# One core, two attention parts: the end of the global part handed to the local part piece by piece

## The chip, the cores and the metric

The kernel runs on one core of a Trainium2 chip. Its time is device microseconds per execution, the median of a few; the profile is one more execution, taken with the hardware profiler. Engines are named as the profile names them: PE (TensorE, matmuls and transposes), DVE (VectorE), ACT (ScalarE), POOL (GpSimd), SP (SyncE, which issues most DMAs). All data is float32.

## What is computed

For x of shape (2, 2048, 256), with `ln` the layer normalization without weights:

```python
xn  = ln(x)
s   = global_attention(xn) + ln(xn) * gamma + beta   # 16 heads of 16, a spatial bias on 256 keys, softmax over 2048
g   = silu(ffn(xn))                                  # two layers, below
out = x + s * g
# one ffn layer: shift half of the channels by one token; q, k, v = h @ wqkv (8 heads of 64);
# l2norm and rotary on q, k; attention in windows of 128 with the window before;
# x += o @ wo; shift, layer norm, h @ w1, a * gelu(g), x += h @ w2
```

The global part (s) and the local part (g) both read xn. The last step multiplies them.

## The kernel before

`gated_recurrent_kernel` first calls `global_attention` (L152), then `ffn_branch` (L792). Each opens its own pools of tiles in SBUF and its own pool of the eight PSUM banks (`ps_r` at L167, `ps_f` at L804), and inside each the order of work is written out by hand: what the functions emit is what the engines' queues get, in that order.

**The global part** works through 32 units (batch, group of four heads, 512 queries) in periods of `PATTERN`: tiles of maxima (P, L419 with DVE's L422), of scores (S, L463 with ACT's exponential at L465), sums over values (V, L481) and single pieces of other work (X), taken from the list `others`. Behind the last period three things are left for the last unit: `sums` turns the sums and divides them by their row sum (transposes pd, L564; DVE L567 and L575), `turn_back` turns them back (transposes pr, L584; ACT copy oc, L586), and `project` is called twice (matmuls px, L592; DVE adds them to s at L597, and behind the second SP sends s to DRAM, L599). L684 runs what remains of `others`.

**The local part** goes over 64 tiles of 128 tokens (16 slots of 512), layer by layer. Before its first tile it clears on POOL `u_last` (L814), two `k_ring` (L817) and six `sm` (L820), whose zeros at the edges are read later, and loads weights (`load_o`, `load_1`, `load_2`, L1207 to L1209). In step n the order of pieces is a list of letters, `FIRST_STEP` for n up to 8 and then `STEP`:

- Q, K, V: the projections of tile n (L889). For Q and K DVE multiplies by rotary tables (L906 to L908), ACT squares (sqq, L910), POOL adds (L911); one piece later DVE sums the squares (L915, L919) and POOL takes the root by a power (L920) and scales (L921). For V ACT copies (L895).
- T0, T1: the turning of Q and K of tile n - 1 (transposes L934; ACT copies xT at L938, DVE copies K into `k_ring` at L943).
- S0, S1: the scores of tile n - 1 (L962; DVE masks and takes maxima at L976, ACT exponentials at L984; one piece later the scaling, for the first eight tiles on ACT, L995).
- W0, W1, A0, A1: the weights of tile n - 2 turned (L1013; copies pT at L1019) and the sums over values (L1036; ACT copies oT, L1044).
- R, F, G: pieces of the feed-forward block of earlier slots (L1051, L1067 to L1091, L1127 and on).

`bank` hands out the eight PSUM banks in turn. `load_tables` (L709) loads the rotary tables of a slot on SP and multiplies them by scales on POOL (L718); for the first layer it is called at the start of steps 1, 3 and 5.

Of the kernel before, what the change touches and what calls it, by code (L numbers as in the profile page):

```python
# [11 lines left out]
F32 = mybir.dt.float32  # L12
# [6 lines left out]
P = 128  # L19
# [23 lines left out]
@with_exitstack  # L43
def gated_recurrent_kernel(ctx: ExitStack, tc: tile.TileContext, t: dict, out: bass.AP):
    nc = tc.nc

    xf = t["x"].rearrange("b n d -> (b n) d")
    x_ch = xf.rearrange("(c t p) d -> c p t d", t=TPC, p=P)
    out_ch = out.rearrange("b n d -> (b n) d").rearrange("(c t p) d -> c p t d", t=TPC, p=P)

    const = ctx.enter_context(tc.tile_pool(name="const", bufs=1))


    ident = const.tile([P, P], F32, name="ident")
    make_identity(nc, ident)
    eps_t = const.tile([P, 1], F32, name="eps_t")
    nc.gpsimd.memset(eps_t, EPS)
    mean_w = const.tile([P, P], F32, name="mean_w")
    nc.gpsimd.memset(mean_w, 1.0 / D)

    vecs = const.tile([P, DEPTH, 2 * NM + 6], F32, name="vecs")
    b2_row = const.tile([P, D], F32, name="b2_row")


    xA = [const.tile([P, 2, N + 1], F32, name=f"xA{b}") for b in range(B)]
    for b in range(B):
        nc.gpsimd.memset(xA[b][:, :, 0:1], 0.0)
    dram = ctx.enter_context(tc.tile_pool(name="dram", bufs=1, space=bass.MemoryType.DRAM))
    s_out = [dram.tile([P, TPC, D], F32, name=f"s_out{c}") for c in range(B * NCH)]

    s_pool = ctx.enter_context(tc.tile_pool(name="s", bufs=1))
    weights = ffn_weights(tc, t, const, s_pool)
    early = [
        lambda: nc.sync.dma_start(vecs, t["vecs"]),
        lambda: nc.sync.dma_start(b2_row, t["b2"][DEPTH - 1 : DEPTH, :].to_broadcast([P, D])),
    ] + [lambda: weights[1](0), lambda: weights[3](0), lambda: weights[2](0, 0)]

    s_all = [s_pool.tile([P, NT, D], F32, tag=f"s{b}", name=f"s{b}") for b in range(B)]
    global_attention(tc, t, xA, s_all, s_out, ident, eps_t, x_ch, early)
    ffn_branch(tc, t, xA, s_out, weights, ident, eps_t, mean_w, vecs, b2_row, x_ch, out_ch)  # L80


# [68 lines left out]

def global_attention(tc, t, xA, s_all, s_out, ident, eps_t, x_ch, early):  # L152

# [10 lines left out]
    with ExitStack() as ctx:  # L164
        cp = ctx.enter_context(tc.tile_pool(name="ga_c", bufs=1))
        p2 = ctx.enter_context(tc.tile_pool(name="ga_2", bufs=2))
        psr = ctx.enter_context(tc.tile_pool(name="ps_r", bufs=1, space=PSUM))  # L167

# [60 lines left out]
        nc.gpsimd.memset(mhalf, -0.5)  # L229
        wp = cp.tile([P, NPR, D], F32, name="wp")  # L230
        for h in range(NG * GH):
# [9 lines left out]
        rings = dict(FIRST_RINGS)  # L241

        def bank(name, shape=(P, CH), ring=None):
            ring = ring or other_ring[0]
            turn[ring] += 1
            tags = rings[ring]
            return psr.tile(list(shape), F32, tag=tags[turn[ring] % len(tags)], name=name)
# [97 lines left out]
        qkv = {}  # L345

        def prep_qk(pi, n, c):
            b, pr = divmod(pi, NPR)
            ps = bank(f"pp_{pi}_{c}_{n}")
            for k in range(2):  # L350
                nc.tensor.matmul(  # L351
                    ps, w[n][:, k, pr * P : (pr + 1) * P], xA[b][:, k, 1 + c * CH : 1 + (c + 1) * CH],
                    start=(k == 0), stop=(k == 1),
                )
            st = p2.tile([P, CH], F32, tag="stage", name=f"stage_{pi}_{c}_{n}", bufs=2)
            nc.scalar.activation(st, ps, AF.Copy, scale=HD ** -0.5 if n == "wq" else 1.0)
            qk_d[pi, n, c] = dram.tile([P, CH], F32, name=f"qk_{pi}_{n}_{c}")
            nc.sync.dma_start(qk_d[pi, n, c], st)
# [113 lines left out]
        def sum_piece():  # L472
# [12 lines left out]
            if kt == 0:  # L485
                os[n] = p2.tile([P, CH], F32, tag="o", name=f"o_{n}")
                nc.scalar.copy(os[n], po)
# [31 lines left out]
        def spread_sums(n, o):  # L519
# [6 lines left out]
            if r == 0:  # L526
                ocs[key] = p2.tile([P, CH], F32, tag=f"on{qc}", name=f"oc_{b}_{g // 2}_{qc}", bufs=1)
            for j in range(GH):
# [30 lines left out]
        def sums(n, o):  # L559
# [3 lines left out]
            for i in range(TPC):  # L563
                nc.tensor.transpose(ps[:, i, :], o[:, i * P : (i + 1) * P], ident)  # L564
            rd = p2.tile([P, TPC, GH, 1], F32, tag="rd", name=f"rd_{n}")
            po = ps.rearrange("p i (j d) -> p i j d", d=HP)
            nc.vector.reciprocal(rd, po[:, :, :, HD : HD + 1])  # L567
            if g % 2 == 0:
                ons[b, g, qc] = p2.tile(
                    [P, TPC, PH, HD], F32, tag=f"on{qc}", name=f"on_{b}_{g // 2}_{qc}", bufs=1  # L570
                )
            on = ons[b, g - g % 2, qc]
# [8 lines left out]
        def turn_back(b, pr, qc, on):  # L581
            ps = bank(f"pr_{b}_{pr}_{qc}")
            for i in range(TPC):
                nc.tensor.transpose(ps[:, i * P : (i + 1) * P], on[:, i].rearrange("p h d -> p (h d)"), ident)  # L584
            o = p2.tile([P, CH], F32, tag="stage", name=f"oc_{b}_{pr}_{qc}", bufs=2)
            nc.scalar.copy(o, ps)  # L586
            others[:0] = [lambda: project(b, pr, qc, o, 0), lambda: project(b, pr, qc, o, 2)]
# [94 lines left out]
        while waiting:  # L682
            pass_place()
        while others:  # L684
            others.pop(0)()

# [94 lines left out]


STEP = "T0 T1 W0 W1 S0 S1 A0 A1 R Q K V F G G G".split()

FIRST_STEP = "Q T0 W0 W1 T1 R K A0 A1 S0 G S1 V F G G".split()
N_FIRST = 8
N_SM = 6
# [3 lines left out]

def ffn_branch(tc, t, xA, s_out, weights, ident, eps_t, mean_w, vecs, b2_row, x_ch, out_ch):  # L792

# [7 lines left out]
    with ExitStack() as ctx:  # L801
        cp = ctx.enter_context(tc.tile_pool(name="ff_c", bufs=1))
        pool = ctx.enter_context(tc.tile_pool(name="ff", bufs=2))
        psr = ctx.enter_context(tc.tile_pool(name="ps_f", bufs=1, space=PSUM))  # L804

# [7 lines left out]
        u_last = cp.tile([P, CH], F32, name="u_last")  # L813
        nc.gpsimd.memset(u_last, 0.0)  # L814
        k_ring = [cp.tile([P, 4, 3 * P], F32, name=f"k_ring{b}") for b in range(B)]
        for k in k_ring:
            nc.gpsimd.memset(k[:, :, P : 2 * P], 0.0)  # L817
        sms = [cp.tile([P, 2, 2 * HD2 + WIN], F32, name=f"sm{i}") for i in range(N_SM)]
        for sm in sms:
            nc.gpsimd.memset(sm, 0.0)  # L820
        next_sm = [0]
        ctx.enter_context(tc.manual_schedule())

        turn = [0]

        def bank(name, shape=(P, CH)):
            turn[0] += 1
            return psr.tile(list(shape), F32, tag=f"f{turn[0] % 8}", name=name)

# [254 lines left out]
        def f_var(s):  # L1084
# [3 lines left out]
            nc.tensor.matmul(pw, mean_w, sq[:, 0, :], start=True, stop=True)  # L1088
            rs = pool.tile([P, CH], F32, tag="rs", name=f"rs_{s}", bufs=1)
            def root():  # L1090
# [16 lines left out]
        def f_var_at(s, n, places):  # L1107
# [3 lines left out]
            for (dn, op), f in zip(places, todo):  # L1111
                hook(n + dn, op, f)

        def f_gate(s, m, n):

# [14 lines left out]
            if n == 1:  # L1130
                gl = pool.tile([P, CH], F32, tag="gl", name=f"gl_{nm}")
                nc.scalar.activation(gl[:mw], ps[:mw], AF.Gelu, bias=V[:mw, NM + m : NM + m + 1])  # L1132
# [8 lines left out]
        def f_last(s, m, mw):  # L1141
# [5 lines left out]
            for k in range(2):  # L1147
                nc.tensor.matmul(ps, W["1 last"][:, k, :], hc[:, k, :], start=(k == 0), stop=(k == 1))
            gl = pool.tile([P, CH], F32, tag="gl", name=f"gl_{s}_{m}")
            h = P // 2  # L1150
# [6 lines left out]
        def f_out(s, k, part):  # L1157
# [16 lines left out]
            if part == 0:  # L1174
                F["py"] = bank(f"pz_{s}_{k}", (P, 2, D))
                F["xt"] = bank(f"pzx_{s}_{k}", (P, 2, D))
                F["s"] = pool.tile([P, 2, D], F32, tag="s", name=f"s_{s}_{k}", bufs=1)
                F["x"] = pool.tile([P, 2, D], F32, tag="x", name=f"x_{s}_{k}", bufs=1)
                F["y"] = pool.tile([P, 2, D], F32, tag="y", name=f"y_{s}_{k}")
                nc.sync.dma_start(F["s"], s_out[b * NCH + cc][:, 2 * k : 2 * k + 2, :])  # L1180
# [25 lines left out]
        gates = []  # L1206
        load_o(0)  # L1207
        load_1(0)
        load_2(0)  # L1209
# [13 lines left out]
        for n in range(len(tiles) + 4):  # L1223
            s, i = divmod(n, TPC)
            cur, pre, pre2 = (tiles[x] if 0 <= x < len(tiles) else None for x in (n, n - 1, n - 2))
            order = FIRST_STEP if n <= N_FIRST else STEP

# [29 lines left out]
            if i == 0 and s % B == 0 and B <= s <= per_layer:  # L1257
                if s == B:
                    load_scales(1)
                load_tables(1, s // B - 1)  # L1260
            if n in (1, 3, 5):
                load_tables(0, (n + 1) // 2)
            if i == 0 and s == per_layer:
# [8 lines left out]
            for op in order:  # L1272
# [7 lines left out]
                elif op[0] in "WA":  # L1280
                    if pre2:
                        piece(lambda: (a_weights if op[0] == "W" else a_sums)(*pre2, j))
                elif op == "R":
                    if i == 0 and have(s - 2):
# [14 lines left out]
                for f in hooks.pop((n, op), []):  # L1299
                    f()  # L1300

            if s == per_layer and i == 1:
                load_o(1)
# [112 lines left out]
```

## Time and profile before

| what | value |
| --- | --- |
| median of three runs | 3050.07 us (3047.15 to 3050.91) |
| the profiled execution's own time | 3048.12 us |
| its span, first to last instruction | 3046.3 us |
| mean granted TensorE clock | 0.991 |
| busy: PE, DVE, ACT, POOL | 2972.1, 2198.3, 2131.6, 1609.2 us |
| last transposes pd of the global part | 1678.05 us |
| its last matmuls px | 1680.92 us |
| first projection of the local part | 1683.69 us |
| first transposes of the local part | 1693.63 us |

Times of day in the text are microseconds from the span's start. In the profile's lines "out<-in" names tiles; L is the line of the kernel; "A <- B" in a list of waits means that A stood idle until B was done. PE's records of a float32 matmul come in pairs, two for an instruction. A busy PE is not a PE at its peak.

### The profile page before, as it was taken

How to read it: one execution, taken by the hardware profiler on the slowest of the kernel's cores; microseconds unless marked ns; L12 is line 12 of the kernel's file. 1: busy time of each engine (PE TensorE's matmuls, PEld its weight loads, DVE VectorE, ACT ScalarE, POOL GpSimd, SP SyncE). 2: the span in 40 equal slices, each digit the busy share in tenths (PEclk: the TensorE clock that was granted, in tenths of full speed). 3: DMA queues.
4: the chain of work that ended last, by engine and by line, in shares of the span. 5: the costliest groups of instructions: out<-in, count | busy, mean ns of one | idle time of the engine just before them, and what ended most of it. 6: DMA issues, size and time to landing. Idle time of an engine off the chain costs nothing.

```text
span 3046.3 us, 60013 instructions
## 1 busy us (share of the span) xinstructions
PE 2972.1 (98%) x22348; PEld 1340.3 (44%) x22348; DVE 2198.3 (72%) x4792; ACT 2131.6 (70%) x4524; POOL 1609.2 (53%) x1454
## 2 busy tenths in 40 slices
PE   8999999999999999999999889999999999999998
PEld 3433333333333333333333455555555555555565
DVE  6898888788887788888884556666666666666653
ACT  3788878788887788888888565555555655665652
POOL 3575435456543354444542746656666556666642
PEclk9999999999999999999999989999999999999999
DMA  3100101000001100000000200000000000000001
GB/s 121 30 14 18 28 19 30 26 12 21 21 25 45 50 19 14 14 25 7 7 10 27 71 10 1 8 1 8 1 29 8 1 21 17 22 22 22 22 22 55
DMA packets 65847, 70.62 MB, mean 23 GB/s; under 512 B 28744, under 2 KB 44188, under 8 KB 65556
## 3 DMA queue, kind: packets, MB, share of 16 engines
q1 hardware_dynamic: 64658, 66.00, 7.2%
q8 instruction: 177, 2.90, 0.4%
q14 instruction: 114, 0.93, 0.1%
q10 hardware_dynamic: 386, 0.52, 0.0%
q0 software_dynamic: 512, 0.26, 0.0%
HBM read 45.26 MB, written 17.53 MB: 21 GB/s over the span
## 4 chain that ended last, share of the span: by engine, by line
PE 88%; DVE 3%; ACT 3%; issue 3%; POOL 1%; DMA 1%; SPq 0%; POOLq 0%; DVEq 0%; ACTq 0%
PE pm L419 18%; PE po L481 16%; PE ps L463 14%; PE pp L889 10%; PE pg L1127 7%; PE po L1036 3%; PE px L1051 3%; PE ps L962 3%; PE py L1166 3%; PE pz L1185 2%; PE pw L1013 1%; ACT sm L984 1%; PE px L592 1%; PE pp_wk L351 1%; PE pv L385 1%
## 5 line engine op out<-in xcount | busy, mean ns | idle before, releaser
L422 DVE TENSOR_REDUCE mx<-pm 128x1 f32<-128x512 f32 x2048 | 1270.3, 683 | 218.0 <-PE ps L463 207.3
L465 ACT ACTIVATE e<-ps 128x512 f32<-128x512 f32 x2048 | 1058.2, 603 | 246.2 <-PE ps L463 245.5
L419 PE MATMUL pm<-kT,qT 32*128 32x512 f32 x4096 | 1020.0, 616 | 4.8 <-DVE mx L422 4.6
L463 PE MATMUL ps<-qa,kT 32*128 32x512 f32 x4096 | 1013.1, 615 | 0.0
L493 POOL TENSOR_TENSOR o<-o,part 128x512 f32<-128x512 f32 x465 | 589.5, 1268 | 777.4 <-ACT part L492 772.4
L419 PEld LDWEIGHTS pm<-kT,qT 32*128 32x128 f32 x4096 | 402.7, 183 | 409.9 <-DVE mx L422 385.2
L481 PE MATMUL po<-e,v 128*32 128x512 f32 x4096 | 546.3, 605 | 0.0
L463 PEld LDWEIGHTS ps<-qa,kT 32*128 32x128 f32 x4096 | 397.1, 183 | 187.1 <-ACT e L465 107.3
L998 POOL TENSOR_TENSOR sm<-sm,wls 128x384 f32<-128x384 f32 x224 | 180.3, 826 | 396.7 <-DVE wls L990 389.0
L889 PE MATMUL pp<-weights,xA 128*128 128x512 f32 x768 | 357.0, 613 | 0.8 <-DVE s L597 0.8
L492 ACT COPY part<-po 128x512 f32<-128x512 f32 x465 | 287.0, 617 | 6.4 <-PE po L481 5.2
L1127 PE MATMUL pg<-hc,weights 128*128 128x512 f32 x640 | 284.8, 592 | 0.0
L481 PEld LDWEIGHTS po<-e,v 128*32 128x32 f32 x4096 | 81.0, 108 | 389.4 <-ACT e L465 359.8
L984 ACT ACTIVATE sm<-sm,wmx 128x192 f32<-128x192 f32 x512 | 225.4, 441 | 6.1 <-DVE wmx L976 5.5
L920 POOL TENSOR_TENSOR rn<-rn,mhalf 128x8 f32<-128x8 f32 x128 | 215.6, 1684 | 15.1 <-DVE rn L919 10.9
L889 PEld LDWEIGHTS pp<-weights,xA 128*128 128x128 f32 x768 | 143.7, 193 | 170.3 <-issue 167.9
L910 ACT ACTIVATE sqq<-pp 128x512 f32<-128x512 f32 x128 | 76.3, 596 | 176.9 <-DVE swp L908 148.2
L1127 PEld LDWEIGHTS pg<-hc,weights 128*128 128x128 f32 x640 | 121.1, 190 | 150.2 <-issue 145.7
L911 POOL TENSOR_TENSOR rot<-rot,swp 128x512 f32<-128x512 f32 x128 | 163.3, 1289 | 31.0 <-DVE swp L908 30.9
L1136 DVE SCALAR_TENSOR_TENSOR u<-pg,vecs,gl 128x512 f32<-128x512 f32 x80 | 59.9, 748 | 151.4 <-ACT gl L1132 74.2
L976 DVE CUSTOM_DVE_ANT_0 sm<-ps,mask 128x192 f32<-128x192 f32 x512 | 147.0, 352 | 3.1 <-PE ps L962 2.7
L990 DVE RECIPROCAL wls<-wls 128x4 f32<-128x4 f32 x128 | 22.8, 178 | 174.4 <-ACT sm L984 174.3
(177 smaller groups left out, 3409.8 us busy)
## 6 DMA issues: line engine op xcount, KB each, us to landing
s<-in_x_dram SPq DMA_DIRECT2D x8, 512.0 KB
qk_wk<-stage_wk SPq DMA_DIRECT2D x16, 256.0 KB
kT<-qk_wk SPq DMA_DIRECT2D x128, 32.0 KB
qk_wq<-stage_wq SPq DMA_DIRECT2D x16, 256.0 KB
qT<-qk_wq SPq DMA_DIRECT2D x128, 32.0 KB
qa<-qk_wq SPq DMA_DIRECT2D x128, 32.0 KB
s_out<-s SPq DMA_DIRECT2D x8, 512.0 KB
s<-s_out SPq DMA_DIRECT2D x16, 256.0 KB
```

Source lines behind the costliest of these rows:

```text
L419: nc.tensor.matmul(ps, qT[rows, q0 : q0 + P], kT[rows, c * CH : (c + 1) * CH], start=True, stop=True)
L422: nc.vector.tensor_reduce(mxs[n][:, j * TPC + i, c : c + 1], ps, AX.X, ALU.max)
L463: nc.tensor.matmul(ps, kT[rows, kt * P : (kt + 1) * P], qas[n % 2][rows, :], start=True, stop=True)
L465: nc.scalar.activation(e, ps, AF.Exp)
L481: nc.tensor.matmul(po[j * HP : (j + 1) * HP, :], v[:, kt, (r + j) * VW : (r + j) * VW + HP], es.pop((n, kt, j)), start=True, stop=True,)
L492: nc.scalar.copy(part, po)
L493: nc.gpsimd.tensor_add(os[n], os[n], part)
L889: nc.tensor.matmul(ps, xA[b][:, k, at : at + P], W["qkv"][:, k, n * INNER : (n + 1) * INNER], start=(k == 0), stop=(k == 1),)
L920: nc.gpsimd.tensor_tensor(rn, rn, mhalf, ALU.pow)
L984: nc.scalar.activation(sm[:, x, IN], sm[:, x, IN], AF.Exp, scale=-1.0, bias=mx[:, hb, r, x : x + 1], accum_out=ls[:, hb, r, x : x + 1],)
L998: nc.gpsimd.tensor_mul(sm, sm, ls[:, hb, r, :, None].to_broadcast([P, 2, WIN]))
L1127: nc.tensor.matmul(ps[:mw], W["1"][:, k, at : at + mw], hc[:, k, :], start=(k == 0), stop=(k == 1))
```

## The change

The PSUM pool and a pool of shared SBUF tiles (`both`) are opened once, outside, and handed to both parts. The global part's tiles that its end needs (`wp`, `stage`, `o`, `oc`, `on`, `rd`) come from the shared pool, in the local part `rs`, `gl`, `s`, `x` and `y` do. `global_attention` no longer empties `others` but returns `left`, which runs its next piece with the local part's `bank`. The first two local steps get lists of their own, in which X runs such a piece; K of the second tile goes in front of T0. The clears move from POOL to ACT as multiplications by 0.0 of a broadcast column, one half behind step 0 and one behind step 1. `load_o` and `load_1` move behind step 1, `load_tables` behind steps 3, 5 and 7.

```diff
+    psr = ctx.enter_context(tc.tile_pool(name="ps", bufs=1, space=PSUM))
+    both = ctx.enter_context(tc.tile_pool(name="both", bufs=1))
+    def shared(i, shape, name):
+        return both.tile(list(shape), F32, tag=f"both{i}", name=name)
-        while others:
-            others.pop(0)()
+        def left(bank):
+            other_bank[:] = [bank]
+            if others:
+                others.pop(0)()
+            return bool(others)
+        return left
...
+BANKS = ["s0", "s1", "s2", "s3", "p0", "p1", "p2", "p3"]
+START_STEPS = ["Q X K X V X".split(), "Q X K X X T0 T1 S0 S1 V F".split()]
...
-        nc.gpsimd.memset(u_last, 0.0)
-        for k in k_ring:
-            nc.gpsimd.memset(k[:, :, P : 2 * P], 0.0)
-        for sm in sms:
-            nc.gpsimd.memset(sm, 0.0)
+        def clear(n):
+            first = [k_ring[0][:, :, P : 2 * P]] + sms[:4]
+            for x in first if n == 0 else [k_ring[1][:, :, P : 2 * P]] + sms[4:] + [u_last]:
+                zero = ident[:, :1] if len(x.shape) == 2 else ident[:, None, :1]
+                nc.scalar.mul(x, zero.to_broadcast(list(x.shape)), 0.0)
...
-        load_o(0)
-        load_1(0)
         load_2(0)
...
-            order = FIRST_STEP if n <= N_FIRST else STEP
+            order = START_STEPS[n] if n < 2 else FIRST_STEP if n <= N_FIRST else STEP
...
-            if n in (1, 3, 5):
-                load_tables(0, (n + 1) // 2)
...
+                elif op == "X":
+                    left(bank)
...
+            if n < 2:
+                clear(n)
+            if n in (3, 5, 7):
+                load_tables(0, n // 2)
+            if n == 1:
+                while left(bank):
+                    pass
+                load_o(0)
+                load_1(0)
```

More of the change, by code (lines that the diff above doesn't have):

```diff
@@ L78, in gated_recurrent_kernel @@
     s_all = [s_pool.tile([P, NT, D], F32, tag=f"s{b}", name=f"s{b}") for b in range(B)]
-    global_attention(tc, t, xA, s_all, s_out, ident, eps_t, x_ch, early)
-    ffn_branch(tc, t, xA, s_out, weights, ident, eps_t, mean_w, vecs, b2_row, x_ch, out_ch)
+    psr = ctx.enter_context(tc.tile_pool(name="ps", bufs=1, space=PSUM))
+    both = ctx.enter_context(tc.tile_pool(name="both", bufs=1))
+    def shared(i, shape, name):
+        return both.tile(list(shape), F32, tag=f"both{i}", name=name)
+    left = global_attention(tc, t, xA, s_all, s_out, ident, eps_t, x_ch, early, psr, shared)
+    ffn_branch(
+        tc, t, xA, s_out, weights, ident, eps_t, mean_w, vecs, b2_row, x_ch, out_ch, psr, shared, left
+    )
 def spatial_bias(tc, t, pool, tmp, **how):
@@ L149, with global_attention @@
 ).split()
-def global_attention(tc, t, xA, s_all, s_out, ident, eps_t, x_ch, early):
+def global_attention(tc, t, xA, s_all, s_out, ident, eps_t, x_ch, early, psr, shared):
     nc = tc.nc
@@ L166, in global_attention @@
         p2 = ctx.enter_context(tc.tile_pool(name="ga_2", bufs=2))
-        psr = ctx.enter_context(tc.tile_pool(name="ps_r", bufs=1, space=PSUM))
         ones_col = cp.tile([P, 1], F32, name="ones_col")
@@ L229, in global_attention @@
         nc.gpsimd.memset(mhalf, -0.5)
-        wp = cp.tile([P, NPR, D], F32, name="wp")
+        wp = shared(4, (P, NPR, D), "wp")
         for h in range(NG * GH):
@@ L241, in global_attention @@
         rings = dict(FIRST_RINGS)
+        other_bank = []
         def bank(name, shape=(P, CH), ring=None):
+            if other_bank:
+                return other_bank[0](name, shape)
             ring = ring or other_ring[0]
@@ L345, in global_attention @@
         qkv = {}
+        staged = [0]
         def prep_qk(pi, n, c):
@@ L354, in prep_qk @@
                 )
-            st = p2.tile([P, CH], F32, tag="stage", name=f"stage_{pi}_{c}_{n}", bufs=2)
+            staged[0] += 1
+            if staged[0] % 2:
+                st = shared(6, (P, CH), f"stage_{pi}_{c}_{n}")
+            else:
+                st = p2.tile([P, CH], F32, tag="stage", name=f"stage_{pi}_{c}_{n}", bufs=1)
             nc.scalar.activation(st, ps, AF.Copy, scale=HD ** -0.5 if n == "wq" else 1.0)
@@ L485, in sum_piece @@
             if kt == 0:
-                os[n] = p2.tile([P, CH], F32, tag="o", name=f"o_{n}")
+                if n % 2:
+                    os[n] = shared(5, (P, CH), f"o_{n}")
+                else:
+                    os[n] = p2.tile([P, CH], F32, tag="o", name=f"o_{n}", bufs=1)
                 nc.scalar.copy(os[n], po)
@@ L526, in spread_sums @@
             if r == 0:
-                ocs[key] = p2.tile([P, CH], F32, tag=f"on{qc}", name=f"oc_{b}_{g // 2}_{qc}", bufs=1)
+                ocs[key] = shared(qc, (P, CH), f"oc_{b}_{g // 2}_{qc}")
             for j in range(GH):
@@ L564, in sums @@
                 nc.tensor.transpose(ps[:, i, :], o[:, i * P : (i + 1) * P], ident)
-            rd = p2.tile([P, TPC, GH, 1], F32, tag="rd", name=f"rd_{n}")
+            rd = shared("rd", (P, TPC, GH, 1), f"rd_{n}")
             po = ps.rearrange("p i (j d) -> p i j d", d=HP)
@@ L568, in sums @@
             if g % 2 == 0:
-                ons[b, g, qc] = p2.tile(
-                    [P, TPC, PH, HD], F32, tag=f"on{qc}", name=f"on_{b}_{g // 2}_{qc}", bufs=1
-                )
+                ons[b, g, qc] = shared(qc, (P, TPC, PH, HD), f"on_{b}_{g // 2}_{qc}")
             on = ons[b, g - g % 2, qc]
@@ L584, in turn_back @@
                 nc.tensor.transpose(ps[:, i * P : (i + 1) * P], on[:, i].rearrange("p h d -> p (h d)"), ident)
-            o = p2.tile([P, CH], F32, tag="stage", name=f"oc_{b}_{pr}_{qc}", bufs=2)
+            o = shared(6, (P, CH), f"oc_{b}_{pr}_{qc}")
             nc.scalar.copy(o, ps)
@@ L789, with ffn_branch @@
 LAST_ROOT = [(0, op) for op in ("F", "G0", "G0", "G1", "G1")] + [(0, "G2"), (1, "T0")]
-def ffn_branch(tc, t, xA, s_out, weights, ident, eps_t, mean_w, vecs, b2_row, x_ch, out_ch):
+def ffn_branch(
+    tc, t, xA, s_out, weights, ident, eps_t, mean_w, vecs, b2_row, x_ch, out_ch, psr, shared, left
+):
     nc = tc.nc
@@ L803, in ffn_branch @@
         pool = ctx.enter_context(tc.tile_pool(name="ff", bufs=2))
-        psr = ctx.enter_context(tc.tile_pool(name="ps_f", bufs=1, space=PSUM))
         W, load_scales, load_tables, load_qkv, load_o, load_1, load_2 = weights
@@ L813, in ffn_branch @@
         u_last = cp.tile([P, CH], F32, name="u_last")
-        nc.gpsimd.memset(u_last, 0.0)
         k_ring = [cp.tile([P, 4, 3 * P], F32, name=f"k_ring{b}") for b in range(B)]
-        for k in k_ring:
-            nc.gpsimd.memset(k[:, :, P : 2 * P], 0.0)
         sms = [cp.tile([P, 2, 2 * HD2 + WIN], F32, name=f"sm{i}") for i in range(N_SM)]
-        for sm in sms:
-            nc.gpsimd.memset(sm, 0.0)
-        next_sm = [0]
+        next_sm = [-1]
         ctx.enter_context(tc.manual_schedule())
+        def clear(n):
[3 more added lines that the diff above has]
+                nc.scalar.mul(x, zero.to_broadcast(list(x.shape)), 0.0)
         turn = [0]
@@ L827, in bank @@
             turn[0] += 1
-            return psr.tile(list(shape), F32, tag=f"f{turn[0] % 8}", name=name)
+            return psr.tile(list(shape), F32, tag=BANKS[turn[0] % 8], name=name)
         later = []
@@ L1088, in f_var @@
             nc.tensor.matmul(pw, mean_w, sq[:, 0, :], start=True, stop=True)
-            rs = pool.tile([P, CH], F32, tag="rs", name=f"rs_{s}", bufs=1)
+            rs = shared(4, (P, CH), f"rs_{s}")
             def root():
@@ L1112, in f_var_at, with next_gl @@
                 hook(n + dn, op, f)
+        turn_gl = [0]
+        def next_gl(nm):
+            turn_gl[0] += 1
+            return shared(5 + turn_gl[0] % 2, (P, CH), f"gl_{nm}")
         def f_gate(s, m, n):
@@ L1130, in f_gate @@
             if n == 1:
-                gl = pool.tile([P, CH], F32, tag="gl", name=f"gl_{nm}")
+                gl = next_gl(nm)
                 nc.scalar.activation(gl[:mw], ps[:mw], AF.Gelu, bias=V[:mw, NM + m : NM + m + 1])
@@ L1148, in f_last @@
                 nc.tensor.matmul(ps, W["1 last"][:, k, :], hc[:, k, :], start=(k == 0), stop=(k == 1))
-            gl = pool.tile([P, CH], F32, tag="gl", name=f"gl_{s}_{m}")
+            gl = next_gl(f"{s}_{m}")
             h = P // 2
@@ L1176, in f_out @@
                 F["xt"] = bank(f"pzx_{s}_{k}", (P, 2, D))
-                F["s"] = pool.tile([P, 2, D], F32, tag="s", name=f"s_{s}_{k}", bufs=1)
-                F["x"] = pool.tile([P, 2, D], F32, tag="x", name=f"x_{s}_{k}", bufs=1)
-                F["y"] = pool.tile([P, 2, D], F32, tag="y", name=f"y_{s}_{k}")
+                F["s"] = shared(0, (P, 2, D), f"s_{s}_{k}")
+                F["x"] = shared(1, (P, 2, D), f"x_{s}_{k}")
+                F["y"] = shared(2 + k, (P, 2, D), f"y_{s}_{k}")
                 nc.sync.dma_start(F["s"], s_out[b * NCH + cc][:, 2 * k : 2 * k + 2, :])
```

## The prediction, made before the changed kernel had run

> **What bounds the kernel now.** I read the strip of 40 slices first. It shows an almost full TensorE (PE) everywhere; it is thinner only at the start, at the end and in slices 23 and 24, where the global part hands over to the local part.
>
> ```profile
> span 3046.3 us, 60013 instructions
> ...
> PE   8999999999999999999999889999999999999998
> ```
>
> The table of stretches gives the size: PE is busy for 20.00 of 20 us in 1640 to 1660, but for 7.68 of 10 in 1674 to 1684, 7.19 of 10 in 1684 to 1694, 7.97 and 8.08 in the next two; from 1884 on it is above 97%. So time saved at the handover is kept to the end: what follows is PE's own work and merely starts earlier. Next I read the chain that ended last through the handover (start, length, engine, line):
>
> ```profile
> 1680.92 2.01 PE px L592 x8
> 1682.97 0.52 POOL u_last L814
> 1683.50 0.93 POOL k_ring L817 x2
> 1684.42 2.76 POOL sm L820 x5
> ...
> 1696.35 0.69 PE pt L934 x5
> 1697.04 3.58 PE pp L889 x4
> 1700.64 0.69 DVE rot L906
> ...
> 1705.14 1.06 ACT sm L984 x5
> 1706.20 1.38 ACT sm L995 x4
> 1707.95 1.49 ACT sm L995 x4
> 1709.45 0.49 ACT sqq L910
> 1709.98 0.46 PE pt L934 x7
> ```
>
> The reader is to see that the end of the global part (px, and pr and oc ahead of it at 1679.61 and 1680.28) and the clearing on POOL stand in line before the first rotated Q and K (pt); that K1 (the 3.58) stands before the first scores; and that afterwards ScalarE (ACT) leads: eight exponentials (L984), eight scalings (L995), then the squares of Q2 (sqq), for which PE waits. The list of waits of 1677 to 1714 says why (waiter, awaited: us, times, longest):
>
> ```profile
> POOL u_last L814 <- PE px L592: 22.4, 1, 22.4
> ...
> DVE rot L906 <- POOL sm L820: 2.6, 1, 2.6
> ```
>
> and PE's own list, 1677 to 1860:
>
> ```profile
> PE pt L934 <- ACT sqq L910: 1.2, 1, 1.2
> ...
> PE pp L889 <- DVE s L597: 0.8, 1, 0.8
> ```
>
> All but the third are pools given back: nothing local starts until the global part's last read. The third is a PSUM bank: T1 of step 2 takes the bank that Q2 filled, eight allocations back.
>
> I call Q0, K0, V0 the projections of the first local tile, Q1 to V1 those of the second; T0 and T1 the turning of Q and K, S the scores, W the turning of the weights.
>
> **The change part by part.** In the built program the five engines' orders up to the last pieces of the global part are unchanged, so nothing before 1677 is costed. There are as many buffers of each shared name as before (stage, o, y and gl two, the others one), hence no new reuse distance: 0.
>
> *Q0 moves up.* PE's order becomes pd, Q0, pr, px, K0, px, V0, Q1, K1, T0, T1, S0, S1, V1. Q0 has no wait. pd is issued by 1678.55; a projection takes four records of 0.427 (16 records from 1683.69 to 1690.5), 1.71 together: Q0 ends at 1680.26. The transposes pr, ready at 1679.61, stand behind it and go at 1680.26, 0.65 late; so do oc and px (1681.57). Then px 0.85, K0 1.71 to 1684.13, its result 0.16 later. This stretch (PE idle for 2.3 us of 1674 to 1684) is where the two streams fill each other's holes.
>
> *POOL is freed.* The nine clears at 1682.97 to 1687.87 leave POOL, and its first addition need not wait till 1688.34. What releases T1 now: K0's result 1684.29, three DVE multiplications 1.36 (1690.87 to 1692.21 for the same group), so 1685.7; then POOL adds K0 (pitch 1.23), powers Q0 (1.72), scales Q0 (1.0), powers K0 (1.72), scales K0 (1.05): 1692.45. T1 was at 1696.35: 3.9 earlier. PE has finished K1 by 1690.1, so it waits for this.
>
> *K1 moves in front of T0.* The 3.58 between T1 and S0 goes. What is late next is the copy into k_ring: T1 0.7, first copy 0.4, so S0 really runs from about 1694.0 instead of 1700.53: 6.5 earlier. DVE has K1's rotation behind it, while before the first L976 stood behind it until 1701.91; from start of scores to the first L984 I take 1.33 (1793.72 to 1795.05, undisturbed) instead of 2.07. L984 starts at 1695.3 against 1702.60: **7.3 us earlier**. From there to the squares of Q2 the order on ACT is as before, 6.75 (1702.60 to 1709.35), so ACT comes to them at 1702.05. V1 and Q2 are through PE by 1698.9.
>
> *The clears move to ACT.* The first five stand behind v0 (1686.9), the last four exactly behind the last L995, in front of the squares of Q2, xT and pT. No row shows ACT clearing from a broadcast source. The nearest, SBUF to SBUF, are these two, each from the listing of its line (shortest, median and longest in ns):
>
> ```profile
> L995 ACT ACTIVATE sm<-sm,wls x64: 437/441/457, 1706.1 to 1821.2; 128x192 f32<-128x192 f32 x64
> ```
> ```profile
> L1081 ACT ACTIVATE sq<-hc x16: 1040/1057/1058, 1802.3 to 2982.6; 128x1024 f32<-128x1024 f32 x16
> ```
>
> Between them 0.73 ns an element; with the pitch of L995, 0.346, I get 0.67 for 640 and 0.58 for 512 elements. The first five cost 3.3: they end at 1690.7, before the squares of K1 could start (1691.7): hidden by the POOL chain. The last four cost 2 x 0.67 + 2 x 0.58 = **2.5, on the path**: T1 of step 2 waits for the squares of Q2. These come at 1704.55 against 1709.35: of 7.3, 4.8 is left. Bounds for a clear of 640: 0.35 (L995, size ignored) and 1.47 (256 elements in 0.589 at L286, taken in proportion). I take 0.67, from the two rows nearest in kind. The lower end makes the four 1.4 and the gain 5.9; the upper end is the slower rival below.
>
> *From step 2 on* each step starts from the one before (K of tile n, rotation, squares, sums, L984, L995, squares of Q of tile n+1), so the 4.8 is carried. The multiplication of the rotary tables moves from steps 1, 3, 5 to 3, 5, 7. In step 1 it hid under K1: gain 0. Behind step 7 the two (2.5) come just ahead of those of the next layer (1797.73 to 1800.24), so POOL is free at 1802.75 for an addition that began at 1801.46; behind it is the sum of squares L1082 (start 1803.42), for which PE waited 1.8. It would start at about 1804.05: **0.65 lost**.
>
> *DMA queues.* On SP the load of w2 passes s_out (issued near 1677.5, its 640 KB on the way while nothing else is); the last s_out goes near 1687.1 instead of 1683.7, and wo and w1, behind it, about 3.4 us later than 1687.17. Their first readers are at 1762.9 and 1839.3: cover of over 70 us. ACT's one DMA issue (1.42) now precedes oc, from 1677.2, and is over by 1678.7: 0. The clear of the w1 tail on POOL waits for that s_out, but stands behind K1's scaling at about 1700: 0.
>
> Sum: -7.3 + 2.5 + 0.65 = -4.15 on the profiled execution's 3048.12 (1.8 outside its span): 3043.97. That execution is 1.95 below the median 3050.07 of three; the four times of before have a mean of 3049.06, which gives 3044.9. I forecast the middle, **3044.4**, 5.7 us or 0.19% below the median.
>
> [...] Trace first: behind holes with transposes alone the granted clock falls (mean 0.68 in 1694 to 1704): K1 and K5 (1753.39) took 3.6 to 3.8, K4 (1739.67) and K6 (1774.21) 1.9 to 2.0. K2 is slow there already (3.57), so the sum stands. [...]
>
> **The rivals.**
> 1. *The last clears are hidden or nearly free.* For it: PE reaches T0 and W0 by 1699.5, and 3 us of its wait is slack. Against it: the wait for sqq, and ACT's strict order. Price: the full 7.3 less 0.65, 3048.12 - 6.65 = 3041.5.
> 2. *The clock gives it back.* K4 and K6 ran at full clock and K3 (2.99) and K8 (3.18) partly; if all four came out like K5's 3.78, 1.8 + 1.85 + 0.8 + 0.6 = 5.05 would be lost: 3049.4. For it: the clock's mean is below 1 in ten of the fifteen stretches between 1684 and 1884. Against it: they can also fall better; and 3047.15 to 3050.91 bounds what they did in before.
> 3. *It does not do what it says*: a pool's release still holds Q0, or the scores wait for something else; then only K1's place counts, and some 1 us is left: 3047 to 3048. Against it: Q0 has no wait in the built program.
> 4. *Slower: ACT's clears become the bound.* With c for a clear of 640, the first five end at 1687.4 + 4.86c, and once c exceeds 0.75 the squares of K1, k_ring and S0 wait for them; the squares of Q2 then come at 1698.5 + 8.58c. That decides from c = 1.27, where 1709.35 is reached. At the upper row, 1.47, they come at 1711.1, and with the 0.65 the time is 3050.5; at c = 2, past any row, 3056.
>
> **How the numbers follow.** About 0.2%, 6.1 us, is what a measurement of this kernel can tell from no change: faster is below 3043.97, slower above 3056.2. Forecast 0.55 (0.24 of it faster, 0.31 within, since it lies at the edge); rival 1 0.17 (faster); rival 2 0.16 and rival 3 0.05 (within); rival 4 0.07 (0.03 within, 0.04 slower). So faster 0.41, same 0.55, slower 0.04. The range reaches over rival 1 and nearly all of rival 2: 3040.5 to 3049.
>
> **What would show it.** Right: Q0 within 0.3 us of pd; T1 near 1692.5; L984 from about 1695.3; four ACT clears of 0.6 to 0.8 us just ahead of the squares of Q2, these near 1704.6, and T1 of step 2 right behind. Wrong: clears over 0.9 us, an L984 later than 1697, a second tile's T1 that waits for something other than sqq, or later steps whose count of slow K differs by more than two.

## The result and the profile after

The changed kernel takes **3055.01 us** (median of 13 runs, 3050.91 to 3059.06) against 3047.35 for the kernel before on the same chip (13 runs, 3046.30 to 3051.30): a ratio of **1.0022, 95% interval 1.0014 to 1.0031**. It is slower by about 7 us, where the forecast was 4 to 6 us faster. The profiled execution took 3055.13, its span is 3053.3, its mean clock 0.989.

The strip of the page after. PE's thin slices are again 23 and 24, and the second of them (1755.6 to 1832) is thinner than before, which already points behind the handover:

```profile
span 3053.3 us, 60006 instructions
...
PE   8999999999999999999999879999999999999998
```

The chain through the handover, after (start, length, engine, line, count):

```profile
1677.82 0.44 PE pd L584 x4
1678.25 1.72 PE pp L917 x4
...
1684.80 5.16 PE pp L917 x12
...
1694.00 3.17 PE ps L990 x30
...
1701.80 1.40 ACT sm L1023 x4
1703.20 0.09 ACT k_ring L850
1703.29 0.33 issue
1703.62 1.35 ACT sm L850 x2
1704.96 0.52 ACT u_last L850
1705.48 0.49 ACT sqq L938
1706.02 0.66 PE pt L962 x7
1706.68 3.34 PE pp L917 x4
```

The handover does what it says. Q0 (the first 1.72) follows pd at once; POOL's clears are gone from the chain; the scores start at 1694.00 instead of 1700.53; the last clears stand on ACT ahead of the squares. K2 starts at 1706.61 (PE's listing) instead of 1710.37. This execution reached pd 0.50 earlier, so 3.26 are won. PE's list of waits from 1677 to 1860 agrees: the wait of Q0 for the global part's last read is gone, and T1 of step 2 waits 2.4 for the squares (the longest of the two in the second line):

```profile
PE pv L1116 <- POOL sq L1110: 11.1, 1, 11.1
PE pt L962 <- ACT sqq L938: 3.6, 2, 2.4
```

At K7 (1784.37 against 1787.52) 2.65 are left. So the loss comes later. The table of stretches of PE (start and end, length, busy with the number of records, clock, DMA share, GB/s) finds it, before and then after:

```profile
1794.00:1804.00 10.00, 8.18 (x90) 1.00 0.10 31
1804.00:1824.00 20.00, 15.04 (x146) 0.81 0.00 1
```
```profile
1794.00:1804.00 10.00, 4.28 (x53) 0.88 0.15 43
1804.00:1824.00 20.00, 11.53 (x90) 0.72 0.04 13
```

PE loses 7.4 busy us in these 30. The chain of after says what it waited for:

```profile
1793.88 0.55 POOL k_ring L973
1794.44 2.48 POOL rt L742 x2
1796.92 0.02 issue
1796.93 0.33 SPq L728
...
1798.26 4.80 DMA sc<-in_k_scale_dram
...
1803.13 2.13 issue
...
1805.30 0.60 POOL weights L742
...
1807.77 1.22 POOL rot L939
1808.99 1.23 POOL sq L1110
1810.22 0.04 issue
1810.26 2.07 PE pv L1116 x2
```

Read it from the end. PE's variances (pv) wait for POOL's sum of squares; POOL stands at the multiplication of the *next* layer's rotary tables (`weights`, L742); that waits for DMAs. The first of them in SP's queue, the load of the scales `sc` (`load_scales(1)`, L728), could not be issued before POOL's *last* multiplication for the first layer (`rt`, 1794.4 to 1796.9) was done, because `sc` has one buffer and that multiplication still reads it. The change had put that multiplication behind step 7.

The waits of SP's queue from 1780 to 1815, before and then after, and that of PE for pv before (after: the 11.1 above):

```profile
SPq L716 <- DVE rot L906: 38.9, 1, 38.9
```
```profile
SPq L728 <- POOL rt L742: 92.6, 1, 92.6
```
```profile
PE pv L1088 <- POOL sq L1082: 1.8, 1, 1.8
```
Before, the loads of the scales were issued at 1750.35 to 1753.05, and SP waited only to load the tables into their old place, once DVE had done with it: issued at 1792.06, multiplied at 1797.73. After, the tables stand behind the scales in SP's queue and go at 1799.74. POOL's listing of after shows the hole (the last bracket is the idle time ahead and what ended it):

```profile
1794.39 2.51 POOL L742 TENSOR_TENSOR rt<-rt,sc 128x512 f32<-128x512 f32 x2
1805.29 2.48 POOL L742 TENSOR_TENSOR weights<-weights,sc 128x512 f32<-128x512 f32 x2 [8.38 <-DMA weights<-in_rot_dram]
1807.73 1.26 POOL L939 TENSOR_TENSOR rot<-rot,swp 128x512 f32<-128x512 f32 x1
1808.95 1.26 POOL L1110 TENSOR_TENSOR sq<-sq 128x512 f32<-128x512 f32 x1
```

Counted from the start of the last pd, after minus before is: K2 -3.26, K7 -2.65, pv +6.02, the last matmuls (pz) +7.51. From K7 to pv of step 8 alone 8.7 are lost.

### The profile page after: what moved, and what is told of

Read it like the earlier page. It is cut to its first block, busy times and chain, and to the rows that moved or that the text cites. A ratio compares the mean times of both kernels' runs of the same rounds, so it can differ in the third digit from the quotient of the medians.

```text
span 3053.3 us, 60006 instructions
## 1 busy us (share of the span) xinstructions
PE 2973.1 (97%) x22348; PEld 1341.6 (44%) x22348; DVE 2198.6 (72%) x4792; ACT 2136.8 (70%) x4533; POOL 1604.7 (53%) x1445
## 4 chain that ended last, share of the span: by engine, by line
PE 89%; DVE 3%; issue 3%; ACT 2%; DMA 1%; POOL 1%; SPq 0%; POOLq 0%; DVEq 0%; ACTq 0%
PE pm L436 18%; PE po L498 16%; PE ps L480 14%; PE pp L917 10%; PE pg L1161 7%; PE po L1064 3%; PE px L1079 3%; PE ps L990 3%; PE py L1200 3%; PE pz L1219 2%; PE pw L1041 1%; PE px L610 1%; PE pp_wk L364 1%; PE pv L402 1%; PE pt L962 1%
## 5 line engine op out<-in xcount | busy, mean ns | idle before, releaser
L1012 ACT ACTIVATE sm<-sm,wmx 128x192 f32<-128x192 f32 x512 | 225.3, 441 | 10.1 <-DVE wmx L1004 9.4
```

Of the source, the lines that this page charges most:

```text
L1012: nc.scalar.activation(sm[:, x, IN], sm[:, x, IN], AF.Exp, scale=-1.0, bias=mx[:, hb, r, x : x + 1], accum_out=ls[:, hb, r, x : x + 1],)
```

## The experiments

The theory: the moved tables hold back the scales' load, through the single buffer of `sc`, and that is the whole reversal; without it the handover gains about what the forecast's other terms say. The rivals: two more multiplications on POOL in step 7 are the harm, whatever SP does; or the clock, or the clears on ACT. The table counts from the start of the last pd in each profiled execution, so that what differs ahead of it does not enter; one execution stands behind each row's three columns, and the profiled ones are not always near the median (before357's is the longest of its seven, gap2scales' the shortest of its nine). Ratio and interval are against the kernel before on the same chip; they use all executions, so a ratio is not the quotient of the two medians.

| kernel | median us | ratio (95%) | K2 | pv, step 8 | last pz |
| --- | --- | --- | --- | --- | --- |
| before | - | 1 | 32.22 | 126.59 | 1358.93 |
| after | 3055.01 | 1.0022 (1.0014 to 1.0031) | 28.96 | 132.61 | 1366.44 |
| tables135 | 3044.95 | 0.9990 (0.9981 to 0.9999) | 29.00 | 123.37 | 1356.34 |
| twoscales | 3045.18 | 0.9987 (0.9978 to 0.9996) | 28.77 | 121.76 | 1355.62 |
| before357 | 3057.95 | 1.0029 (1.0019 to 1.0040) | 32.99 | 134.47 | 1368.52 |
| gapclear | 3040.25 | 0.9968 (0.9955 to 0.9980) | 26.72 | 119.22 | 1351.54 |
| poolclear | 3045.09 | 0.9982 (0.9973 to 0.9991) | 26.40 | 120.24 | 1353.48 |
| endfirst | 3044.83 | 0.9980 (0.9972 to 0.9989) | 28.90 | 121.64 | 1353.98 |
| klater | 3049.34 | 0.9996 (0.9988 to 1.0005) | 31.36 | 121.30 | 1354.45 |
| fillv | 3041.80 | 0.9976 (0.9965 to 0.9986) | 25.66 | 118.56 | 1351.43 |
| gap2scales | 3038.30 | 0.9974 (0.9964 to 0.9984) | 26.62 | 115.39 | 1348.91 |
| fill2scales | 3041.46 | 0.9978 (0.9969 to 0.9986) | 25.65 | 120.86 | 1352.90 |

The kernel before had a median of 3049.03 beside tables135, twoscales, before357 and gapclear, 3049.85 beside poolclear, endfirst, klater and fillv, 3048.80 beside the last two.

**tables135**: the changed kernel with the tables at the ends of steps 1, 3 and 5.

```diff
-            if n in (3, 5, 7):
-                load_tables(0, n // 2)
+            if n in (1, 3, 5):
+                load_tables(0, (n + 1) // 2)
```

> The changed kernel with one edit: the rotary tables are multiplied behind steps 1, 3 and 5 instead of 3, 5 and 7. Theory (the late multiplication of step 7 holds the scales' one tile, so that the next layer's scales are loaded and waited for): the wait of 11.1 us of pv for the sum of squares falls to about 2, so 9.3 us go: about 3045.7, faster than before by 1 to 3 us. Rival (the handover itself or a clock that stays low costs the time): nothing of it moves, 3052 or more.

**twoscales**: the changed kernel, tables where the change puts them, but the second layer's scales in a tile of their own.

```diff
-        sc = own.tile([P, 2, 2, HD2], F32, tag="sc", name=f"sc_{l}")
+        sc = own.tile([P, 2, 2, HD2], F32, tag=f"sc{l}", name=f"sc_{l}")
```

> The changed kernel with one edit: the scales of the second layer get a tile of their own; the tables stay behind steps 3, 5 and 7. Theory: the load of the scales no longer waits, only POOL's 2.5 us more in front of the sum of squares is left, 0.65 to 2.5 us: 3046 to 3048. If instead POOL's place of the multiplication alone is the cost, it stays near 3055. Rival (handover or clock): 3052 or more.

**before357**: the kernel before with its tables behind steps 3, 5 and 7, nothing else.

```diff
-            if n in (1, 3, 5):
-                load_tables(0, (n + 1) // 2)
 ...
+            if n in (3, 5, 7):
+                load_tables(0, n // 2)
```

> The kernel before with one edit: the tables are multiplied behind steps 3, 5 and 7. Theory: it gets the same stall by itself, about 9 us: 3056 against 3047.4. Rival (handover or clock): within 1 us of before.

These three settle the cause. In before357 the late tables alone cost the kernel before 0.29%, with the same waits, SP's queue and PE:

```profile
SPq L704 <- POOL rt L718: 101.8, 1, 101.8
```
```profile
PE pv L1088 <- POOL sq L1082: 10.2, 1, 10.2
```

Taking them back (tables135), or leaving them and taking away only the shared buffer (twoscales), both give some 10 us back; twoscales came 0.8 below its expected range. In twoscales the waits of SP's queue, 1780 to 1830, have no load of the scales any more, only the tables', for DVE:

```profile
SPq L740 <- DVE rot L934: 234.6, 2, 157.0
```

PE's wait in step 8, tables135 and then twoscales:

```profile
PE pv L1116 <- POOL sq L1110: 1.8, 1, 1.8
```
```profile
PE pv L1116 <- POOL sq L1110: 2.7, 1, 2.7
```

The second rival is thereby priced: POOL's two multiplications in step 7 make the wait 0.9 longer, not 9.3. The columns pv and pz hold the lengths of the projections as well: twoscales stands 1.6 ahead of tables135 at pv in spite of the longer wait, and its K3 and K4 took 3.25 and 1.98, those of tables135 3.78 and 3.63. The median of tables135 is 4.1 us below the kernel before beside it, where the forecast without its 0.65 said 4.8. That is in part luck: the interval reaches from 0.3 to 5.8 us, and in the trace K2 comes 3.2 and the last pz 2.6 earlier than before.

**gapclear**: tables135 with the second half of the clears ahead of S0 of step 1, where ACT stood idle for 3.8 us, instead of behind the step.

```diff
+                if n == 1 and op == "S0":
+                    clear(1)
 ...
-            if n < 2:
+            if n < 1:
                 clear(n)
```

> As tables135, and the second half of the clears stands in front of the first scores instead of behind the last scaling of step 1, where ACT waits for 3.75 us anyway. If the clears are on the path as forecast (2.4 us between the last scaling and the squares of Q2), it is 2 to 2.5 us faster than tables135: about 3043.4. If they are hidden, it is the same as tables135.

ACT's wait for the first maxima, 1690 to 1706, in tables135 and then in gapclear:

```profile
ACT sm L1012 <- DVE wmx L1004: 3.8, 1, 3.8
```
```profile
ACT sm L1012 <- DVE wmx L1004: 1.5, 1, 1.5
```

The clears went into that wait, and K2 came 2.3 earlier. It also took 1.99 instead of 3.35 us, and K4 1.98 instead of 3.63 (granted clock 0.92 against 0.84 in 1696 to 1716, 0.93 against 0.79 in 1716 to 1740). The time gained is larger than expected (4.7 us by the medians), and these faster projections go with it; that the place of the clears brought them about was not tried by itself.

**poolclear**: tables135 with the clears as `nc.gpsimd.memset(x, 0.0)` at the same places (behind steps 0 and 1).

> tables135 with the nine clears as memsets on POOL instead of copies of zeros on ACT, at the places where the changed kernel has them (behind step 0 and step 1). If what the last four clears cost is their place in ACT's queue ahead of the squares of Q2 (2.5 us), that goes: 3044.95 - 2.5 = 3042.5, or 3040.5 if K2 also runs at full clock as in gapclear. Rival: POOL is just as much in the way (it rotates and adds for T2), and the time is that of tables135, 3045, or more.

The median is the rival's 3045, but the kernel before was slower beside this run than beside tables135, and the two ratios (0.9982 and 0.9990) with their intervals leave the expected 2.5 us open as well. The trace shows both halves: K2 comes as early as in gapclear (26.40), so it was ACT's queue that the clears blocked, and then the scores of step 2 wait for POOL, which has its last clears (2.1) and the two multiplications of the tables (2.5) ahead of K's copy; in gapclear, with the tables alone there, that wait is 1.0. PE's waits, 1677 to 1720:

```profile
PE ps L989 <- POOL k_ring L972: 3.9, 1, 3.9
```

**endfirst, klater, fillv** are gapclear with another order of pieces in the first steps:

```diff
-START_STEPS = ["Q X K X V X".split(), "Q X K X X T0 T1 S0 S1 V F".split()]
+START_STEPS = ["X X X Q K V".split(), "Q X K X X T0 T1 S0 S1 V F".split()]   # endfirst
+START_STEPS = ["Q X K X V X".split(), "Q X X X T0 T1 K S0 S1 V F".split()]   # klater
+START_STEPS = ["Q X K X V X".split(), "Q X K X X T0 V T1 S0 S1 F".split()]   # fillv
```

> gapclear with the end of the global part handed over whole at the start of step 0 (three pieces, then Q0, K0, V0), not between Q0, K0 and V0. If the order of the pieces is what pays: K0 issues behind the last two px instead of ahead of them, about 2.1 us later, T1 and S0 follow, and the time is about 2 us above gapclear's 3040.25: 3042.3. Rival: only the shared pools and Q0 right behind pd matter, T1 waits for something else, and the time stays within 0.5 us of gapclear.

K2 comes 2.2 later than in gapclear, and the last pz 2.4 later: in the trace the order of the end's pieces is worth what was expected. The times alone do not show it: the median is 4.6 above gapclear's, and the intervals overlap.

> gapclear with K1 between T1 and S0 in step 1, as in the kernel before, instead of ahead of T0. If moving K1 in front of T0 fills time in which TensorE would wait for the rotated T0, the first L1012 comes about 2.3 us later and the time is about 3042.5. Rival: S0, which ran cold at 3.15 us behind the hole ahead of T1, is moved behind K1 and runs at full clock at 1.5 us, and the two cancel: within 0.7 us of gapclear.

Neither number held. S0 and S1 (here and below "S0", the 32 records of both) did run faster (1.86 instead of 3.16) and the first wait for T0 did appear (1.39 ahead of T0, 2.26 ahead of T1), but W0 then waited 2.5, K2 took 3.78 (granted clock of 1696 to 1716: 0.76, gapclear 0.92) and the scores of step 2 came at 36.92, as late as before (36.81). The profiled execution wins most of it back by step 8; it is one of the shortest of the eleven (3043.99 to 3051.82), and the median does not show that gain. The intervals of klater and gapclear do not overlap, so K1's place in front of T0 is worth something; how much (9 us by the medians, 2.9 by the last pz), with the clock's part apart, stays open.

> gapclear with V1 put between T0 and T1 in step 1, where TensorE waits for POOL's rotated T1. If the hole ahead of T1 is what makes S0 run cold (3.15 us instead of 1.5), filling it gives S0 back its 1.6 us: about 3038.7. Rival: V1 is the work that now covers the wait behind the exponentials in step 1, and a hole opens there of V1's length (about 2 us), at a cold clock behind it: 3041 to 3043.

S0 took 1.85 instead of 3.16 and K2 came 1.06 earlier, but K2 took 3.78 (granted clock of 1696 to 1716: 0.83, gapclear 0.92): at pv 0.7 is left, at the last pz 0.1. The median lies where the rival had it, and the intervals of fillv and gapclear overlap.

**gap2scales, fill2scales**: gapclear and fillv with the tables behind 3, 5, 7 and the scales' tile of twoscales.

> the two mends together: the second layer's scales in a tile of their own with the tables behind steps 3, 5 and 7 as in the changed kernel, and the second group of clears ahead of S0 of step 1, in ACT's wait. If the late tables hurt only through the scales' tile, the time is that of gapclear, 3040.25, less up to 1.0 us, since POOL's two multiplications (2.5 us) no longer stand ahead of the rotations of step 2, and plus up to 0.9 us for the same two in step 7 ahead of the squares of step 8: 3039.5 to 3041. Rival: late tables hurt by their place on POOL too, and the time is 2 us or more above gapclear.

> gap2scales with V1 between T0 and T1. If V1 ahead of T1 only shortens the hole and the hole that opens behind the exponentials costs as much, the time is that of gap2scales within 1 us, and S0 again runs in 1.85 us or less and K2 at 3.4 or more. Rival: with POOL free of the tables the hole before K2 closes too and the time falls by 1.5 us.

gap2scales has the lowest median of all, 3038.30 (ratio 0.9974, where the changed kernel has 1.0022), 1.2 below its expected range. From gapclear's it cannot be told apart (the ratios' intervals overlap). Its nine executions lie in two groups, five from 3036.17 to 3038.30 at a mean clock of 0.993 and four from 3042.56 to 3043.16 at 0.991; the profiled one is the shortest of the first, so its lead of 3.8 over gapclear at pv cannot be put down to the buffer. With the scales' buffer doubled the late tables do no harm that can be measured. fill2scales has S0 at 1.85 and K2 at 3.37, as its first sentence said, but its time is 3.2 above gap2scales rather than within 1; the overlapping intervals leave the sign open.

## Why the prediction was wrong

The step that failed is *From step 2 on*, "0.65 lost", together with *DMA queues*, which listed the loads that the change delays but not this one. I costed the multiplications that move to behind step 7 as 2.5 us of POOL's own time and asked only who stands behind them on POOL. I did not ask who waits for the tile that they **read**. `load_scales(1)` writes it, and SP's queue stands still behind that load. In place of the 0.65 the runs showed 8.7 from K7 to pv (0.9 of PE's wait is POOL's own time, by twoscales). None of the four rivals had it: rival 4 had the sign right with another mechanism, ACT's clears, which the trace excludes (0.72 for 640 elements, 0.62 for 512). Its last price is also added wrongly: with c = 2 its own formula puts the squares at 1715.7 and the time at 3055.1, not 3056.

The other steps, in the order of the forecast:

- *Q0 moves up*: right. Q0 began 0.44 behind pd, and px came in the order given.
- *POOL is freed*: right. T1 came at 1692.33, 1692.83 on the time of before (all of after is 0.5 earlier up to pd), forecast 1692.45.
- *K1 moves in front of T0*: half right. S0 at 1694.5 on that time, forecast 1694.0. The first L1012 came at 1696.34, so 1696.84, forecast 1695.3: 0.5 from S0's start, 1.0 because S0 took 3.15 where I had taken an undisturbed row (1.53). So 5.8 instead of 7.3.
- *The clears move to ACT*: right. The last four held the squares of Q2 from 1703.10 to 1705.48, 2.4 for a forecast of 2.5; gapclear gives 2.3 of it back. One row was misread on the way: the 1.2 that PE waited for the squares before is at 1773.75, in step 6; from 1700 to 1714 the list of before has no such wait, and only the chain shows the squares of Q2 just ahead of T1.
- *The clock behind holes* was weighed at the hole ahead of K2 only, and there little changed: the hole was 4.8, as before, K2 took 3.40 at a granted clock of 0.58 (before: 3.63 at 0.53), and the sums behind K2 took 1.09 (before: 1.10). But PE has nothing except transposes from 1689.9 to 1694.0, 4.1 us, and S0 behind them took 3.15 at a granted clock of 0.50 (before, behind K1: 1.53 at 1.00). With V1 in that hole (fillv) S0 took 1.85; the granted clock of 1676 to 1696 was 1.00 there and 0.91 in gapclear. What in such a hole lowers the clock was not shown.
- *Sum*: with 5.8 and 2.4 it is -3.4 at K2, where -3.26 was measured. By K7 0.6 of it is gone: the projections K2 to K6 took 15.8 us against 14.4 (granted clock of 1716 to 1740: 0.79 against 0.93), rival 2 in small. Then the 8.7 of step 8 turns it to +6.0. The last 1.5 (from pv to pz) comes behind the stall, where the clock is lower (0.72 against 0.81 in 1804 to 1824, 0.91 against 0.96 in 1824 to 1900); whether the stall caused that was not tried by itself, and in twoscales, with hardly any stall, as much is lost against before from pv to pz (1.5, from the table).

## What to carry to other kernels

When an instruction is moved later, follow its inputs as well as its output and its queue: here a tile that it reads, `sc`, stayed taken until 1796.9, and the next load into its single buffer waited with all that stood behind it in SP's queue (first issue at 1796.93, in the kernel before at 1750.35), in a step far from the handover. The sign of it was a new wait of the DMA queue in the list of waits (from 38.9 on DVE to 92.6 on POOL). Clearing and other work without inputs is to be tried in an idle stretch of the engine that does it (here ACT's 3.8 us, gapclear): at the end of step 1 the clears held the squares of Q2 for 2.4 us.

## What the runs showed of the hardware

Six loads of one row of a scale to 128 partitions, as the kernel before issues them too, took SP 2.7 us to issue; the last landed 6.1 us after the first was issued (1796.93 to 1803.06), for 128 KB in all. All this was hidden before. After, POOL's wait ended not with the scales but 2.2 us later with the tables behind them in the queue, which were issued at 1799.74 and multiplied from 1805.29 on; so the scales cost the late start of SP's queue (1796.93) and the 2.7 us of issuing.

The time of one kernel goes with PE's granted clock, and it spreads more than I had allowed for. klater's eleven executions: 0.993 at 3043.99, 0.992 at 3045.3 to 3045.7, 0.991 at 3047.7 and 3049.3, 0.990 at 3050.4 to 3051.8 (mean clock and time). Edits worth 1 or 2 us locally (fillv, twoscales' 0.9) therefore show in the trace but not in the medians.
